# Second step of a sparse-attention graph layer: five rounds of top values, a slope from a law, and small steps moved to GpSimd

## Chip, cores and metric

One core of one Trainium2 chip runs the whole program. The metric is device time in microseconds (us) from launch to end. The engines are PE (TensorE matmul), PEld (its weight loads), DVE (VectorE), ACT (ScalarE), POOL (GpSimd) and SP (SyncE, which issues DMAs).

## What is computed

For 3327 nodes with 256 features, x is normalised and rectified to h. Then two steps of two diffusions are run over h: one along a sparse adjacency matrix, one along an attention matrix that keeps, in each row, the largest probabilities until their sum reaches 0.9.

```python
for n in range(STEPS):                       # STEPS = 2
    q = Xa @ W1.T @ W2.T; k = Xa @ W3.T
    probs = softmax(q @ k.T)
    A = probs where (sum of the larger ones in the row) < TOP_P else 0     # TOP_P = 0.9
    A = A / A.sum(-1)
    Xf = R @ Xf                              # R = (adj + I), rows normalised
    Xa = A @ Xa
    Z = Z + Xf @ U1[n].T + Xa @ U2[n].T
out = x + layernorm(h + Z)
```

## The kernel before

The nodes are padded to 3328 and cut into 26 tiles of 128 rows. A tile's row of exponentials `e` is 128 x 3328 in float32. Two steps, one after the other, walk over the tiles; in each iteration i of a step's loop, tile i+1 is guessed, tile i is settled and tile i-1 is multiplied, so that several tiles are in flight.

No row is sorted. For each tile, and for each of its 128 rows at once:

- `weights` makes logits on PE (L600) and exponentials on ACT (L604, L608).
- `measured_twice` (second step; `measured_once` in the first) guesses the value at which the larger part of the row's sum is 0.9. A first guess comes from `guessed` (ACT, L620 to L625). Three passes of ACT over `e` (L633, through the helper `through`) measure how much lies under the guess: a Relu, a Sign, and a Sign against a second guess. Between and behind them stand short operations on 128 x 1 columns of a small tile `g` (`col(k)`): on ACT L674 and L675, L687 and L688, L702 to L704; on GpSimd L676 to L678, L689 to L692, L697 and L698, L708 to L712; on DVE L685 and L686, L699 and L700, L706 and L707. L699 reads column 14, which L689 writes. The last exponential, L714 on ACT, gives the final guess, `col(16)`.
- `settle` takes the values under that guess into `w`, with their sum `d2` (L729, on DVE over all 3328 columns). `need` (L730) is what is still to be dropped. The eight largest of each of 20 segments of `w` become 160 candidates (L734). Rounds of a maximum of eight and a replacement (L741, L743) give the largest 48 of them in order in the second step, 40 in the first; a running sum and a comparison with `need` (L748 to L753) give the exact cut. L763 masks `e` with it and sums the row into `ra`, whose reciprocal is L764.
- `Sums` transposes the masked `e` (PE L809, copies by ACT at L811) and multiplies it with the features (`pa`, L823).
- `spread`, `fetched` and `diffuse` gather up to five neighbours' rows by indirect DMAs that GpSimd issues (`xg`, L921) and multiply them (`pr`, L929).
- `finish` (second step) adds up the tile with `ra` (L953, DVE), takes mean and variance (L458, L459), computes the inverse deviation on GpSimd (L465, L466, the second a power) and `nm` (L961), asks for `x` (`xr`, L958, on SP), and then scales, shifts and adds on GpSimd (L968 to L971) and stores (L973).

If any row's cut isn't proved to be right by the candidates (`prove`), a flag makes the program run `search_graph_layer`, which searches by bits, over everything again.

The order of the instructions is written by hand. All of these are generators; an iteration has seven slots, and a string for each slot names by letters which generator goes one stage further: m `measured_twice` of tile i+1, n the same of the tile before (its last stage), d `settle` of tile i, c its last stages an iteration later, f `finish`, g the next gather, s `spread`, w and q `weights`, l the laws. `PLAN[1]` has the second step's strings, `OPEN` those of its first iterations, `LAST` those of its last. At the end every engine's instructions but those of SP in the second step are tied to the order of the text. In the second step's plan the third stage of `finish` (the `xr` load, L465, L466, L961) stands in slot 5, ahead of the part of the guess in slot 6, and one gather stands at the end of slot 6, four in slot 3.

Of the kernel before, what the change touches and what calls it, by code (L numbers as in the profile page):

```python
# [13 lines left out]
AF = mybir.ActivationFunctionType  # L14
ALU = mybir.AluOpType
# [15 lines left out]

SCALE = 1.9
BITS = 27
FIRST = 2.0 ** -7
assert 0.1 * SCALE / N > 2.0 ** -15


# [1 line left out]
def search_graph_layer(  # L39
# [13 lines left out]
    nc = tc.nc  # L53
# [94 lines left out]
    def nucleus(es, z):  # L148
        n = len(es)
        thr = small.tile([P, 2], F32, tag="thr", name="thr")  # L150
        cand = small.tile([P, 2], F32, tag="cand", name="cand")
        ncand = small.tile([P, 2], F32, tag="ncand", name="ncand")
        over = small.tile([P, 2], F32, tag="over", name="over")
        cnt = small.tile([P, 2], F32, tag="cnt", name="cnt")
        mass = small.tile([P, 2], F32, tag="mass", name="mass")
        low = small.tile([P, 2], I32, tag="low", name="low")
        candi = cand.bitcast(I32)
        nc.vector.tensor_scalar(thr, z, TOP_P, None, ALU.mult)
        nc.vector.memset(cand, FIRST)
        for k in range(BITS - 1, -1, -1):  # L160

            nc.vector.tensor_scalar(ncand, cand, -1.0, None, ALU.mult)
            for a in range(n):
                ja = scan.tile([P, NP], U8, tag="ja", name="ja")
                nc.scalar.activation(ja, es[a], AF.Relu, bias=ncand[:, a : a + 1],
                                     accum_out=over[:, a : a + 1])
                jv = scan.tile([P, NP], U8, tag="jv", name="jv")
                nc.vector.tensor_scalar(jv, es[a], cand[:, a : a + 1], None, ALU.is_ge, ALU.add,
                                        accum_out=cnt[:, a : a + 1])
            nc.vector.tensor_tensor(mass, cand, cnt, ALU.mult)  # L170
            nc.vector.tensor_tensor(mass, mass, over, ALU.add)
            nc.vector.tensor_tensor(low, mass, thr, ALU.is_lt)

            nc.vector.tensor_scalar(low, low, k, (1 << k) >> 1,
                                    ALU.logical_shift_left, ALU.bitwise_or)
            nc.vector.tensor_tensor(candi, candi, low, ALU.bitwise_xor)

        rc = small.tile([P, 2], F32, tag="rc", name="rc")  # L180
        nc.vector.reciprocal(rc, cand)
        nc.vector.tensor_scalar(ncand, cand, -1.0, None, ALU.mult)
        lim = small.tile([P, 2], F32, tag="lim", name="lim")
        for a in range(n):
            c = slice(a, a + 1)
            e = es[a]
            nc.vector.scalar_tensor_tensor(e, e, cand[:, c], e, ALU.is_ge, ALU.mult,
                                           accum_out=mass[:, c])
            eq = scan.tile([P, NP], U8, tag="jv", name="eq")
            nc.vector.tensor_scalar(eq, e, cand[:, c], None, ALU.is_equal)  # L190
            nth = scan.tile([P, NP], I16, tag="nth", name="nth")
            nc.vector.tensor_tensor_scan(nth, eq, eq, 0.0, ALU.add, ALU.max)

            nc.vector.tensor_sub(lim[:, c], thr[:, c], mass[:, c])
            nc.vector.scalar_tensor_tensor(lim[:, c], lim[:, c], rc[:, c], nth[:, NP - 1 : NP],
                                           ALU.mult, ALU.add)
            nc.vector.tensor_scalar(lim[:, c], lim[:, c], 1.0, None, ALU.add)
            nc.vector.scalar_tensor_tensor(eq, nth, lim[:, c], eq, ALU.is_ge, ALU.mult)
            nc.vector.scalar_tensor_tensor(e, eq, ncand[:, c], e, ALU.mult, ALU.add)
# [114 lines left out]
LNBIG = 69.0  # L314
SEG = 168
NSEG = -(-NP // SEG)
ROUNDS = (5, 6)
PG = (0.72168716, 3.51308980, -3.48705157)
PK = (3.57528079, -2.54929187, 0.86603878)
OFFSET = (18.0, 14.0)  # L320
TOPK = 8 * max(ROUNDS)
LNY = 0.25 * math.log(0.72)

# [5 lines left out]
HALVES = 7  # L329
FIRST = 8 * P  # L330
CUT = 4
# [14 lines left out]
def guess_graph_layer(ctx, tc, x, adj, w1t, w2t, w3t, u1t, u2t, ln_g, ln_b, out, flag):  # L346
    nc = tc.nc
# [14 lines left out]
    V, G, S, PE = nc.vector, nc.gpsimd, nc.scalar, nc.tensor  # L362
# [46 lines left out]
    half = const.tile([P, 4], F32, tag="half", name="half")  # L409
# [218 lines left out]
    def con(k):  # L628
        return one[:, k : k + 1]
# [38 lines left out]
    def measured_twice(r):  # L668
        e, ms = r["e"], r["ms"]

        col = guessed(r, small.tile([P, 18], F32, tag="g", name="g"))
        S.activation(col(1), col(0), AF.Exp, scale=-1.0, bias=con(5))  # L674
        S.activation(col(11), col(2), AF.Square, bias=con(4))  # L675
        G.tensor_scalar(col(11), col(11), ms(5), ms(6), ALU.mult, ALU.add)  # L676
        G.tensor_scalar(col(5), col(1), OFFSET[1], None, ALU.mult)
        G.tensor_scalar(col(7), col(3), ms(3), ms(8), ALU.mult, ALU.add)  # L678
        yield
        oa = small.tile([P, 3], F32, tag="oa", name="oa")  # L680
        through(e, AF.Relu, col(9), -1.0, oa[:, 0:1])
        yield
        through(e, AF.Sign, col(9), -1.0, oa[:, 1:2])
        yield
        V.tensor_scalar(col(3), oa[:, 1:2], float(NP), col(9), ALU.add, ALU.mult)  # L685
        V.tensor_scalar(col(4), col(3), 0.5, oa[:, 0:1], ALU.mult, ALU.subtract)  # L686
        S.activation(col(6), col(4), AF.Ln, scale=col(1), bias=con(2))  # L687
        S.activation(col(13), col(6), AF.Exp, scale=col(11), bias=col(7))  # L688
        G.tensor_scalar(col(14), col(13), col(9), 0.25, ALU.add, ALU.mult)  # L689
        G.tensor_scalar(col(10), col(13), col(5), 1.0, ALU.mult, ALU.add)  # L690
        G.tensor_scalar(col(8), r["Z"], -0.1, col(4), ALU.mult, ALU.add)
        G.tensor_scalar(col(6), col(6), col(11), col(7), ALU.mult, ALU.add)  # L692
        yield
        through(e, AF.Sign, col(13), -1.0, oa[:, 2:3])
        yield
        d1 = col(17)
        G.tensor_scalar(col(0), oa[:, 2:3], NP - 61.0, BIG, ALU.is_gt, ALU.mult)  # L697
        G.tensor_scalar(col(0), r["Z"], 0.035, col(0), ALU.mult, ALU.add)  # L698
        V.tensor_scalar(col(15), oa[:, 2:3], oa[:, 1:2], col(14), ALU.subtract, ALU.mult)  # L699
        V.tensor_scalar(d1, col(15), col(4), 0.0, ALU.add, ALU.max)  # L700

        S.activation(col(2), d1, AF.Abs, scale=col(1), bias=con(1))  # L702
        S.activation(col(2), col(2), AF.Ln, scale=0.2, bias=col(10))
        S.activation(col(3), d1, AF.Ln, scale=col(1), bias=con(2))  # L704

        V.tensor_scalar(col(12), col(4), d1, 1.0e-30, ALU.subtract, ALU.add)  # L706
        V.reciprocal(col(12), col(12))  # L707
        G.tensor_scalar(col(12), col(12), col(8), 0.7, ALU.mult, ALU.max)  # L708
        G.tensor_scalar(col(11), col(12), 1.5, col(11), ALU.min, ALU.mult)
        G.tensor_tensor(col(2), col(3), col(2), ALU.subtract)  # L710
        G.tensor_scalar(col(15), d1, col(0), LNBIG, ALU.is_lt, ALU.mult)
        G.tensor_tensor(col(6), col(6), col(15), ALU.add)  # L712
        yield
        S.activation(col(16), col(2), AF.Exp, scale=col(11), bias=col(6))  # L714
        yield

    def measured(step, r):
# [5 lines left out]
    def settle(step, t, r):  # L723
        e, col, Z = r["e"], r["col"], r["Z"]
        n = 8 * ROUNDS[step]
        d2 = small.tile([P, 1], F32, tag="d2", name="d2")
        need = small.tile([P, 1], F32, tag="need", name="need")
        w = scan.tile([P, NP], F32, tag="w", name="w")
        V.scalar_tensor_tensor(w, e, col(16), e, ALU.is_lt, ALU.mult, accum_out=d2)  # L729
        V.tensor_scalar(need, Z, -0.1, d2, ALU.mult, ALU.add)  # L730
        yield
        cand = small.tile([P, NSEG * 8], F32, tag="cand", name="cand", bufs=1)
        for s in range(NSEG):
            V.max(cand[:, 8 * s : 8 * s + 8], w[:, s * SEG : min(NP, (s + 1) * SEG)])  # L734
# [26 lines left out]
            V.tensor_tensor(ra, ra, rb, ALU.add)  # L761
        else:
            V.scalar_tensor_tensor(e, e, at(1), e, ALU.is_ge, ALU.mult, accum_out=ra)  # L763
        V.reciprocal(ra, ra)  # L764
        yield
        V.tensor_tensor(cum[:, :n], dr[:, :n], b, ALU.mult)
        V.tensor_reduce(at(2), cum[:, :n], AX.X, ALU.max)

# [357 lines left out]
    def refetch(t):  # L1126
# [7 lines left out]


    PLAN = (("gmdsssa", "gmcdsssa", "edawwpg", "gmsdga", "gmspdea", "ohgdawwqg", "gehmgq"),
            ("llcmss", "lnms", "lwwnfd", "lcmdsssgggg", "fdsmwqdf", "llmdf", "lmwdg"))

    LAST = {NT - 1: ("cfss", "cn", "nd", "sss", "fddddddsf", "f", ""), NT: ("c", "", "", "ff", "ff", "fv", "f"),
            NT + 1: ("fv", "f", "", "", "f", "f", "f")}  # L1140
# [3 lines left out]
             2: ("gmdsssa", "gmcdsssga", "gedawwpg", "gmsdga", "gmspdea", "ohgdawwqg", "gehmgq")}  # L1144
    OPEN = {-1: ("llcmss", "lnms", "lwwnfd", "lcmdsssggggg", "fmgdswqdf", "llmdf", "lmwfdm"),
            0: ("cmssggg", "nms", "wwnfd", "cmdsss", "fdsmgwqdf", "mdf", "mwd"),
            1: ("cmss", "nms", "wwnfd", "cmdsssgggg", "fdsmwqdf", "mgdf", "mwdg")}
    OPEN[2] = OPEN[3] = OPEN[1]
    spacing = itertools.chain(spaced((0, 1)), *(spaced((t,)) for t in range(2, NT)))
    fetching = itertools.chain(*(refetch(t) for t in range(NT)))  # L1150
# [130 lines left out]
```

## Times and profile before

| what | us |
|---|---|
| median of 3 runs | 1354.68 |
| lowest, highest | 1349.92, 1356.13 |
| the profiled execution | 1350.64 |
| its span (first to last instruction) | 1348.9 |
| mean granted TensorE clock | 0.982 |
| PE busy in the span | 1268.1 (94%) |
| DVE busy | 1186.8 (88%) |
| ACT busy | 1081.0 (80%) |
| POOL busy | 997.2 (74%) |

The page divides the span into 40 slices of 33.7 us; the first step ends at about 742 us, with slice 22, and the second fills the rest. A digit is the busy share of a slice in tenths. The page's groups name line, engine, operation, what is written and read, and how often. Timeline lines give start and duration in us, engine, line, operation, operands, and in brackets the idle time ahead of it and what ended it. The ends of matmuls are modelled in the profile, so for PE the spacing of starts is read and not the durations; durations on POOL are rough.

Some of the groups in the second step, from 780 to 1220 us of the span, mean of one:

| line, engine | operation | ns |
|---|---|---|
| L763 DVE | mask and row sum, 3328 columns | 3685 |
| L729 DVE | values under the guess, 3328 columns | 3677 |
| L741 DVE | maximum of eight out of 160 | 323 |
| L743 DVE | replacement of eight in 160 | 309 |
| L730, L706 DVE | column operations | 214 |
| L707, L764 DVE | reciprocal of a column | 164 |
| L633 ACT | one pass over `e` | 3069 |
| L702 ACT | Abs of a column | 387 |
| L466 POOL | power of a column | 579 |
| L690 POOL | column operation | 262 |
| L921 POOL | one indirect DMA (mean; median of all 954) | 1155 |

### The profile page before, as it was taken

The page shows a single profiled execution, that of the slowest core. Times are in us where ns is not written, and L with a number is a line of the kernel's source. Part 1 is how long each engine was busy: PE and PEld are TensorE (multiplying, and loading weights), DVE is VectorE, ACT ScalarE, POOL GpSimd, SP SyncE. Part 2 cuts the span into 40 slices and gives each one's busy share as a digit, 9 for nine tenths or more (in the row PEclk, how much of TensorE's full clock was granted, in tenths as well). Part 3 has the DMA queues.
Part 4 walks back from the last instruction along what each step waited for, and adds up shares of the span by engine and source line. Part 5 has one row for each costly group of instructions (what it writes and reads, how often), then busy time and mean ns, then how long its engine had stood idle before and what let it go on. Part 6 is the DMA issues. An engine that isn't in the chain of part 4 may idle for free.

```text
span 1348.9 us, 22270 instructions
## 1 busy us (share of the span) xinstructions
PE 1268.1 (94%) x6495; PEld 976.0 (72%) x6495; DVE 1186.8 (88%) x3637; ACT 1081.0 (80%) x2368; POOL 997.2 (74%) x1399
## 2 busy tenths in 40 slices
PE   5989899999999999999999579999999999999985
PEld 4635687877778777787877457777777777777774
DVE  6877899999999999999990689899998999999993
ACT  5475788798888879888863789899998999999841
POOL 5114788888878878887873578888888888888832
PEclk9999999999999999999999779999999999999998
DMA  8644545455454544445332212221212222122200
GB/s 277 221 157 141 160 136 144 134 144 147 133 153 133 140 138 142 144 135 152 106 104 86 75 55 60 78 89 54 91 59 85 62 82 90 52 91 64 81 21 24
DMA packets 92645, 149.79 MB, mean 111 GB/s; under 512 B 15425, under 2 KB 59072, under 8 KB 92512
## 3 DMA queue, kind: packets, MB, share of 16 engines
q1 hardware_dynamic: 75056, 105.37, 24.6%
q0 software_dynamic: 16640, 42.69, 12.1%
q8 instruction: 54, 0.88, 0.3%
q14 instruction: 79, 0.65, 0.2%
q10 hardware_dynamic: 816, 0.20, 0.1%
HBM read 120.93 MB, written 27.28 MB: 110 GB/s over the span
## 4 chain that ended last, share of the span: by engine, by line
PE 51%; DVE 20%; ACT 12%; POOL 11%; issue 3%; DMA 2%; SPq 0%; POOLq 0%; DVEq 0%; ACTq 0%
PE pa L823 22%; ACT ja L633 7%; PE pl L600 7%; PE pt L809 6%; PE pr L929 5%; POOL xg L921 5%; DVE w L729 4%; PE pz L942 3%; DVE cand L734 3%; DVE e L763 3%; PE pz L1011 2%; POOL g L676 2%; DVE bb L741 1%; DVE cand L743 1%; ACT e L604 1%
## 5 line engine op out<-in xcount | busy, mean ns | idle before, releaser
L823 PE MATMUL pa<-xw,eT 128*128 128x256 f32 x1352 | 323.6, 384 | 3.6 <-DVE s L953 3.6
L633 ACT ACTIVATE ja<-e,g 128x3328 uint8<-128x3328 f32 x106 | 325.7, 3072 | 0.1
L823 PE MATMUL pa<-x,eT 128*128 128x256 f32 x1352 | 323.1, 380 | 0.0
L823 PEld LDWEIGHTS pa<-xw,eT 128*128 128x128 f32 x1352 | 250.7, 190 | 52.5 <-issue 14.4
L823 PEld LDWEIGHTS pa<-x,eT 128*128 128x128 f32 x1352 | 243.7, 191 | 25.8
L734 DVE MAX8 cand<-w 128x8 f32<-128x168 f32 (+1 forms) x1040 | 253.7, 319 | 0.0
L811 ACT COPY eT<-pt 128x512 f32<-128x512 f32 (+1 forms) x364 | 199.5, 555 | 48.8 <-PE pt L809 47.7
L921 POOL DMA_INDIRECT xg<-bx,index x130 | 188.7, 1451 | 54.7 <-issue 24.4
L900 POOL DMA_INDIRECT ac<-in_adj,index x130 | 162.9, 1253 | 63.8 <-issue 28.2
L809 PE MATMUL pt<-ident,e 128*128 128x128 f32 x1144 | 176.6, 277 | 17.3 <-DVE e L760 9.4
L809 PEld LDWEIGHTS pt<-ident,e 128*128 128x128 f32 x1144 | 139.8, 144 | 60.5 <-issue 36.0
L921 POOL DMA_INDIRECT xg<-vx,index x130 | 152.5, 1173 | 34.3 <-issue 30.3
L729 DVE SCALAR_TENSOR_TENSOR w<-e,g 128x3328 f32<-128x3328 f32 x44 | 162.7, 3698 | 3.1 <-ACT g L714 3.0
L929 PE MATMUL pr<-xg,ac 128*128 128x257 f32 (+1 forms) x520 | 141.0, 395 | 8.4 <-DVE s L1119 6.8
L763 DVE SCALAR_TENSOR_TENSOR e<-e,rec 128x3328 f32<-128x3328 f32 x40 | 148.3, 3707 | 0.6
L604 ACT ACTIVATE e<-pl 128x832 f32<-128x832 f32 x132 | 112.9, 859 | 27.3 <-PE pl L600 21.9
L929 PEld LDWEIGHTS pr<-xg,ac 128*128 128x128 f32 x520 | 93.9, 194 | 34.0 <-issue 14.1
L600 PE MATMUL pl<-both,qT 64*128 64x416 f32 x416 | 93.0, 546 | 9.3 <-ACT e L604 7.0
L741 DVE MAX8 bb<-cand 128x8 f32<-128x160 f32 x286 | 92.7, 324 | 6.4
L853 DVE TENSOR_REDUCE fm<-at 128x4 f32<-128x512 f32 (+1 forms) x133 | 84.7, 637 | 13.3 <-DMA at<-in_adj 13.3
L600 PE MATMUL pl<-after,qT 64*128 64x416 f32 x416 | 95.4, 552 | 0.5 <-ACT e L604 0.5
L633 ACT ACTIVATE ja<-x,g 128x3328 uint8<-128x3328 f32 x24 | 73.7, 3070 | 0.0
(260 smaller groups left out, 2129.8 us busy)
## 6 DMA issues: line engine op xcount, KB each, us to landing
at<-in_adj SPq DMA_DIRECT2D x114, 256.0 KB
cx<-ac SPq DMA_DIRECT2D x26, 384.0 KB
ac<-cx SPq DMA_DIRECT2D x26, 384.0 KB
wide<-in_adj SPq DMA_DIRECT2D x8, 832.0 KB
e<-in_adj SPq DMA_DIRECT2D x6, 832.0 KB
own<-bx SPq DMA_DIRECT2D x26, 128.5 KB
x<-in_x SPq DMA_DIRECT2D x13, 256.0 KB
xr<-in_x SPq DMA_DIRECT2D x26, 128.0 KB
```

The costliest lines, as they stand in the source:

```text
L600: PE.matmul(pl[:, a, :wd], qT[p, :], keys_of(step, a).rearrange("p a b -> p (a b)")[:, c : c + wd], start=True, stop=True)
L604: S.activation(e.rearrange("p (a n) -> p a n", a=2)[:, :, c : c + wd], pl[:, :, :wd], AF.Exp, accum_out=za[:, n : n + 1])
L633: S.activation(ja, e, f, bias=guess, scale=sign, accum_out=total)
L729: V.scalar_tensor_tensor(w, e, col(16), e, ALU.is_lt, ALU.mult, accum_out=d2)
L734: V.max(cand[:, 8 * s : 8 * s + 8], w[:, s * SEG : min(NP, (s + 1) * SEG)])
L763: V.scalar_tensor_tensor(e, e, at(1), e, ALU.is_ge, ALU.mult, accum_out=ra)
L809: PE.transpose(pt[:, j, :], e[:, (j0 + j) * P : (j0 + j + 1) * P], ident)
L811: S.copy(eT[:, :w, :], pt[:, :w, :])
L823: PE.matmul(self.pa, eT[:, c - 4 * k, :], self.xa[:, j, :], start=c == 0, stop=c == NT - 1)
L900: G.indirect_dma_start(out=ac[:, k, :], out_offset=None, in_=rows, in_offset=bass.IndirectOffsetOnAxis(ap=index[:, t, k : k + 1], axis=0), ...
L921: G.indirect_dma_start(out=xg[:, k, :w], out_offset=None, in_=rows, in_offset=bass.IndirectOffsetOnAxis(ap=index[:, t, k : k + 1], axis=0))
L929: PE.matmul(pr[:, :w], ac[:, k, :], own if k == KT - 1 else xg[:, k, :w], start=k == 0, stop=k == KT - 1)
```

## The change

All of it is in the second step.

- `ROUNDS[1]` goes from 6 to 5: the cut is looked for among 40 candidates. `OFFSET[1]` goes from 14 to 24, which sets how far above the expected cut the guess is put.
- The slope with which the guess is corrected is no longer measured (L706 and L707 on DVE, L708 and L709 on GpSimd, with the column of L691) but computed from the law's column 11 by two new operations on GpSimd behind L678, -0.4 col(11)^2 + 0.5 col(11). ACT's Abs (L702) goes; the first of its two logarithms is taken of column 10, which doesn't depend on d1. Three operations on GpSimd stand in place of L708 to L712.
- `need` (L730) and `ra`'s reciprocal (L764, now a power of -1) are computed on GpSimd in the second step, at the beginning of the following stage of `settle`: both in slot 3, behind `finish`'s scaling (L968 to L971, slot 2) and ahead of that slot's four gathers.
- In the second step's plan the third stage of `finish` moves from slot 5 to slot 6, behind the guess's operations there and ahead of the slot's gather.

`FIRST` in the other program is renamed to `LOWEST`.

```diff
--- before.py
+++ after.py
...
@@ -314,10 +314,10 @@
 LNBIG = 69.0
 SEG = 168
 NSEG = -(-NP // SEG)
-ROUNDS = (5, 6)
+ROUNDS = (5, 5)
 PG = (0.72168716, 3.51308980, -3.48705157)
 PK = (3.57528079, -2.54929187, 0.86603878)
-OFFSET = (18.0, 14.0)
+OFFSET = (18.0, 24.0)
 TOPK = 8 * max(ROUNDS)
 LNY = 0.25 * math.log(0.72)
 
@@ -676,6 +676,8 @@
         G.tensor_scalar(col(11), col(11), ms(5), ms(6), ALU.mult, ALU.add)
         G.tensor_scalar(col(5), col(1), OFFSET[1], None, ALU.mult)
         G.tensor_scalar(col(7), col(3), ms(3), ms(8), ALU.mult, ALU.add)
+        G.tensor_scalar(col(12), col(11), -0.4, 0.5, ALU.mult, ALU.add)
+        G.tensor_tensor(col(12), col(12), col(11), ALU.mult)
         yield
         oa = small.tile([P, 3], F32, tag="oa", name="oa")
         through(e, AF.Relu, col(9), -1.0, oa[:, 0:1])
@@ -688,7 +690,6 @@
         S.activation(col(13), col(6), AF.Exp, scale=col(11), bias=col(7))
         G.tensor_scalar(col(14), col(13), col(9), 0.25, ALU.add, ALU.mult)
         G.tensor_scalar(col(10), col(13), col(5), 1.0, ALU.mult, ALU.add)
-        G.tensor_scalar(col(8), r["Z"], -0.1, col(4), ALU.mult, ALU.add)
         G.tensor_scalar(col(6), col(6), col(11), col(7), ALU.mult, ALU.add)
         yield
         through(e, AF.Sign, col(13), -1.0, oa[:, 2:3])
@@ -699,19 +700,13 @@
         V.tensor_scalar(col(15), oa[:, 2:3], oa[:, 1:2], col(14), ALU.subtract, ALU.mult)
         V.tensor_scalar(d1, col(15), col(4), 0.0, ALU.add, ALU.max)
 
-        S.activation(col(2), d1, AF.Abs, scale=col(1), bias=con(1))
-        S.activation(col(2), col(2), AF.Ln, scale=0.2, bias=col(10))
+        S.activation(col(2), col(10), AF.Ln)
         S.activation(col(3), d1, AF.Ln, scale=col(1), bias=con(2))
-
-        V.tensor_scalar(col(12), col(4), d1, 1.0e-30, ALU.subtract, ALU.add)
-        V.reciprocal(col(12), col(12))
-        G.tensor_scalar(col(12), col(12), col(8), 0.7, ALU.mult, ALU.max)
-        G.tensor_scalar(col(11), col(12), 1.5, col(11), ALU.min, ALU.mult)
-        G.tensor_tensor(col(2), col(3), col(2), ALU.subtract)
+        G.tensor_scalar(col(2), col(2), col(12), col(6), ALU.mult, ALU.subtract)
         G.tensor_scalar(col(15), d1, col(0), LNBIG, ALU.is_lt, ALU.mult)
-        G.tensor_tensor(col(6), col(6), col(15), ALU.add)
-        yield
-        S.activation(col(16), col(2), AF.Exp, scale=col(11), bias=col(6))
+        G.tensor_tensor(col(2), col(15), col(2), ALU.subtract)
+        yield
+        S.activation(col(16), col(3), AF.Exp, scale=col(12), bias=col(2))
         yield
 
     def measured(step, r):
@@ -727,8 +722,11 @@
         need = small.tile([P, 1], F32, tag="need", name="need")
         w = scan.tile([P, NP], F32, tag="w", name="w")
         V.scalar_tensor_tensor(w, e, col(16), e, ALU.is_lt, ALU.mult, accum_out=d2)
-        V.tensor_scalar(need, Z, -0.1, d2, ALU.mult, ALU.add)
-        yield
+        if not step:
+            V.tensor_scalar(need, Z, -0.1, d2, ALU.mult, ALU.add)
+        yield
+        if step:
+            G.tensor_scalar(need, Z, -0.1, d2, ALU.mult, ALU.add)
         cand = small.tile([P, NSEG * 8], F32, tag="cand", name="cand", bufs=1)
         for s in range(NSEG):
             V.max(cand[:, 8 * s : 8 * s + 8], w[:, s * SEG : min(NP, (s + 1) * SEG)])
@@ -761,8 +759,11 @@
             V.tensor_tensor(ra, ra, rb, ALU.add)
         else:
             V.scalar_tensor_tensor(e, e, at(1), e, ALU.is_ge, ALU.mult, accum_out=ra)
-        V.reciprocal(ra, ra)
-        yield
+        if not step:
+            V.reciprocal(ra, ra)
+        yield
+        if step:
+            G.tensor_tensor(ra, ra, half[:, 2:3], ALU.pow)
         V.tensor_tensor(cum[:, :n], dr[:, :n], b, ALU.mult)
         V.tensor_reduce(at(2), cum[:, :n], AX.X, ALU.max)
 
@@ -1134,7 +1135,7 @@
 
 
     PLAN = (("gmdsssa", "gmcdsssa", "edawwpg", "gmsdga", "gmspdea", "ohgdawwqg", "gehmgq"),
-            ("llcmss", "lnms", "lwwnfd", "lcmdsssgggg", "fdsmwqdf", "llmdf", "lmwdg"))
+            ("llcmss", "lnms", "lwwnfd", "lcmdsssgggg", "fdsmwqdf", "llmd", "lmwfdg"))
 
     LAST = {NT - 1: ("cfss", "cn", "nd", "sss", "fddddddsf", "f", ""), NT: ("c", "", "", "ff", "ff", "fv", "f"),
             NT + 1: ("fv", "f", "", "", "f", "f", "f")}
@@ -1144,7 +1145,7 @@
              2: ("gmdsssa", "gmcdsssga", "gedawwpg", "gmsdga", "gmspdea", "ohgdawwqg", "gehmgq")}
     OPEN = {-1: ("llcmss", "lnms", "lwwnfd", "lcmdsssggggg", "fmgdswqdf", "llmdf", "lmwfdm"),
             0: ("cmssggg", "nms", "wwnfd", "cmdsss", "fdsmgwqdf", "mdf", "mwd"),
-            1: ("cmss", "nms", "wwnfd", "cmdsssgggg", "fdsmwqdf", "mgdf", "mwdg")}
+            1: ("cmss", "nms", "wwnfd", "cmdsssgggg", "fdsmwqdf", "mgd", "mwfdg")}
     OPEN[2] = OPEN[3] = OPEN[1]
     spacing = itertools.chain(spaced((0, 1)), *(spaced((t,)) for t in range(2, NT)))
     fetching = itertools.chain(*(refetch(t) for t in range(NT)))
```

More of the change, by code (lines that the diff above doesn't have):

```diff
@@ L33 @@
 BITS = 27
-FIRST = 2.0 ** -7
+LOWEST = 2.0 ** -7
 assert 0.1 * SCALE / N > 2.0 ** -15
@@ L158, in nucleus @@
         nc.vector.tensor_scalar(thr, z, TOP_P, None, ALU.mult)
-        nc.vector.memset(cand, FIRST)
+        nc.vector.memset(cand, LOWEST)
         for k in range(BITS - 1, -1, -1):
```

## The prediction

> **What bounds the kernel now.** I read first the page's slices, then windows over the second step, then one settled tile engine by engine in the timeline. Nothing in the first step changes, so the case lies in slices 23 to 40.
>
> ```profile
> PE   5989899999999999999999579999999999999985
> DVE  6877899999999999999990689899998999999993
> ACT  5475788798888879888863789899998999999841
> POOL 5114788888878878887873578888888888888832
> ```
>
> All four engines are busy there, so shares decide nothing. The next lines are windows: length, then busy time of PE, weight loads, DVE, ACT and POOL (instructions), clock, DMA. The first runs over the settled tiles (cut at each tile's first `pa` matmul): 21 tiles, 21.30 us each. The second is one of them.
>
> ```profile
> 831.39:1278.68 447.29, 441.66 (x2267) 343.31 (x2266) 417.61 (x1240) 418.83 (x817) 384.39 (x546) 1.00 0.25 75
> 1153.00:1173.97 20.97, 20.97 (x109) 16.37 (x108) 19.82 (x60) 20.00 (x40) 18.39 (x27) 1.00 0.25 75
> ```
>
> Most tiles take 20.97 to 21.05; two stumble (22.85 from 852, 24.25 from 1023), each with one of 21.6 behind it. In a smooth tile PE is full: its 52 `pa` matmuls start 0.216 us apart, as in the first step where the chain is PE alone, and its one wait is 0.09 to 0.12 us at the first transpose, for L763. PE's own tile is thus 20.87. I call L763 (mask e, sum ra) the cut pass and L729 (values under the guess into w) the guess pass. A loop of DVE and ACT is just as long: from 897 to 999 the chain of waits alternates between these two, at 21.0 a tile. From 1200 to 1275 it names GpSimd, so that comes next, in one tile:
>
> ```profile
> 1220.16 0.24 POOL L677 TENSOR_SCALAR g<-g 128x1 f32<-128x1 f32 x1
> ...
> 1228.65 0.28 POOL L689 TENSOR_SCALAR g<-g 128x1 f32<-128x1 f32 x1
> ...
> 1230.35 0.58 POOL L466 TENSOR_TENSOR rstd<-rstd,half 128x1 f32<-128x1 f32 x1
> 1231.04 0.26 POOL L961 TENSOR_SCALAR nm<-mv,rstd 128x1 f32<-128x1 f32 x1
> ...
> 1233.37 0.19 POOL L712 TENSOR_TENSOR g<-g 128x1 f32<-128x1 f32 x1
> 1233.73 4.35 POOL L921 DMA_INDIRECT xg<-vx,index  x1 [0.17 <-issue]
> 1238.14 2.95 POOL L676 TENSOR_SCALAR g<-g,law 128x1 f32<-128x1 f32 x1
> 1241.15 0.24 POOL L677 TENSOR_SCALAR g<-g 128x1 f32<-128x1 f32 x1
> ```
>
> and DVE beside it:
>
> ```profile
> 1229.54 0.27 DVE L699 TENSOR_SCALAR g<-oa,g 128x1 f32<-128x1 f32 x1 [0.38 <-ACT ja L633]
> ...
> 1233.39 3.69 DVE L763 SCALAR_TENSOR_TENSOR e<-e,rec 128x3328 f32<-128x3328 f32 x1
> 1237.01 0.08 DVE L763 DVE_READ_ACCUMULATOR e<-e,rec 128x1 f32 x1
> 1237.12 0.16 DVE L764 RECIPROCAL ra<-ra 128x1 f32<-128x1 f32 x1
> 1237.20 3.67 DVE L729 SCALAR_TENSOR_TENSOR w<-x,g 128x3328 f32<-128x3328 f32 x1
> ```
>
> GpSimd's queue has no pause. A gather (0.95 us alone) that starts 0.34 us into the cut pass takes 4.35, and L676 (0.34 alone) started in the guess pass ends 0.21 us behind it. Operations that started up to 0.09 us into a pass go through. So a pass shuts GpSimd out, and between two passes one waiting operation slips through. The chain's 4.35 and 2.95 are therefore ends of DVE's passes. The stumbles are the same thing at a worse moment: at 1021 L711, a part of the guess, fell into the cut pass,
>
> ```profile
> 1021.26 3.66 POOL L711 TENSOR_SCALAR g<-g 128x1 f32<-128x1 f32 x1
> ```
>
> and ACT's exponential L714, and with it the guess pass, came late.
>
> **What the Trainium skill says.** "SBUF — State Buffer", section "Who interferes with whom": a VectorE instruction with two SBUF inputs and a GpSimd instruction that reads SBUF exclude each other, and whoever issues first makes the other wait. The trace agrees (waits of 2.6 to 3.4 us). The same section infers that a `tensor_tensor` doesn't stop a GpSimd DMA's descriptor generation; here, under a two-input pass, the gather goes from 0.95 to 4.35, and first-step gathers issued within guess passes end some 0.83 us behind them. "Perfetto Trace Analysis", section "GPSIMD Engine Instruction": time GpSimd by the spacing of starts, not by reported durations; I do. Its section "Identifying the Most-Contended Engine": matmul busy share is no measure of headroom; hence the spacing of matmuls above.
>
> **The change, part by part**, for a settled tile.
>
> DVE loses one round of top values, 0.77 by spacing; L706 and L707, 0.45 (the next maximum follows L700 by 0.13, as one follows L686, instead of 0.58); `need` 0.21; `ra`'s reciprocal 0.1; and about 0.06 on four operations with 40 instead of 48 columns: 1.6 in all. From L699 to the cut pass, 3.85 becomes 2.57. On ACT the Abs goes and the first Ln no longer waits for d1: the work behind comes 0.68 sooner. The DVE-ACT loop falls by 0.9 to 1.6, below PE.
>
> GpSimd gains, ahead of L689: the slope's two operations behind L678, spacings 0.41+0.41+0.17 against 0.31, +0.66; and `ra` (a power like L466) and `need` behind L971, 0.75+0.60+0.44 against 0.88, +0.91. Nothing hides these, since its queue is full: L677 to L689 grows from 8.49 to 10.06. `ra` waits for the cut pass and `need` for the guess pass, both over by then; behind them queue the four gathers and L689. `need` is read 7 us later and `ra` in the next tile by L953, so DVE doesn't wait for these; were `ra` late, L953 would hold DVE and, through `pa`, PE. The gathers' rows are read by PE 20 us after issue. L971's store goes out later on SP by what GpSimd slips, about 2 us, and the loads of `xr`, `sx`, `cx` and `own` stand behind it in the same order as before; the first of them is needed some 14 us on. It loses L691 and swaps L708 to L712 for three operations, 1.0 less, but behind L689, where DVE doesn't wait for it.
>
> DVE waits for L689: L699 reads its column 14. Now L689 ends 9.05 us behind the guess pass's end, and L699 starts at 9.66, after 0.38 of waiting for ACT. Let L677 come w after that end. Then L689 starts at w+10.06, takes 0.28, reaches DVE in about 0.07, 2.57 later the cut pass starts, and both passes take 3.69+0.03+3.67. The loop is w+20.37.
>
> What is w? `rstd`, its power and `nm` (L465, L466, L961) now stand behind the guess. From L689 to L466 I count spacings of 0.24+0.30+0.41+0.36+0.37+0.41+0.37+0.17+0.32 = 2.95. The cut pass starts at 2.92: L466 just gets through, `nm` would start at 3.64, is shut out and takes the gap between the passes, and the fifth gather falls into the guess pass and ends 0.83 behind it; L676 follows at 0.05 and L677 at 0.40 more: w = 1.28. The period is 21.65, against 20.87 for PE and 20.1 for DVE and ACT. GpSimd becomes the bound. The stumbles go, since the guess is done at 2.65.
>
> Sums. Start-up (GpSimd has no finished tile yet): 1.0 at the first guess, 1.3 before the first cut pass, 1.7 from there to the second: -4.0. Settled: a first tile of 20.4, 20 of 21.65, and 2.6 for one pause of GpSimd's queue as at 1012: 456.0 against 447.4, +8.6. End: 0.6 for L712, which runs into the cut pass at 1275, and 1.4 for each of the last two tiles: -3.4. Total +1.2. The profiled execution took 1350.64 (span 1348.9 and 1.7 around it), so 1351.8. It lies 4 us under the median 1354.68 of three runs that spread over 6; from the middle of all four, 1353, I say 1354.
>
> **Rivals.** (1) GpSimd keeps up and PE binds. For it: PE's tile is 20.87, and the stumbles, 6 us, vanish. Against it: `nm` would have to start before the cut pass, 0.6 us earlier than counted. Then 21x20.87 = 438.3: -9.1-4.0-3.4 = -16.5, about 1337. A half-way case, with `nm` just in time by a later cut pass, has period 21.25 and gives 1346. (2) The power L466 misses the cut pass's start, from 0.1 us into it; it has 0.06 to spare. Then it takes the gap, `nm` waits out the guess pass and the gather stands wholly behind: w about 1.7, period 22.1, 465.0 against 447.4, +17.6-7.4 = +10: about 1363, slower. The gap of 0.03 instead of 0.12, with `ra` gone from DVE, could do the same. (3) The guess fails for a row and the second program runs. Worked through on the given inputs, the formulas put the cut within the first 36 of 40 values, so hardly; far over 1400.
>
> **How the numbers follow.** Forecast 0.37, keeping up or half-way 0.34, missed power 0.27, failing 0.02. A measurement can tell 0.5%, 6.8 us, from no change. The added spacings are uncertain by 0.3 us a tile: of the forecast 0.04 ends faster and 0.03 slower, of the half-way case 0.01 is no change, and of the missed power 0.02. Faster 0.37, same 0.33, slower 0.30. The forecast's own range is 1347 to 1360; with most of (1) and (2) it is 1337 to 1366.
>
> **What would show it.** Right: DVE idle before L699's successor with GpSimd as releaser, about 2 us a tile; every fifth gather lasting over 3 us inside the guess pass; PE idle 0.8 a tile; no stumbles. Wrong: tiles of 20.9 with PE never idle (rival 1), or the power lasting over 3 us (rival 2). DVE's busy time per tile should fall by about 1.5 in any case; if not, the count of removed work is wrong.

## The result and the profile after

The changed kernel takes 1358.30 us (median of 20 runs, 1354.05 to 1365.89), the kernel before 1353.31 (20 runs, 1349.60 to 1358.70): ratio 1.0047, 95% interval 1.0031 to 1.0063. It is slower by half a per cent; the forecast was no change. The 1358.30 lies inside the forecast's own range, 1347 to 1360, but with 20 runs of each kernel the interval of the ratio leaves out 1. Runs of either kernel fall into two groups some 6 us apart, and since in the traces of this case the first step, which no kernel here changes, takes either 738 to 740 or 745 to 748 us, medians of a few runs are rough to some us. So I compare the second step of the one profiled execution of each kernel, counted from its first law matmul, L525, to the end: 609.51 us before, 618.16 after.

First the page's slices of the changed kernel, tenths busy:

```profile
DVE  6877799999999999999990698888887888878893
...
POOL 5204788888878878887873588889888888888872
```

DVE has come down from 9 to 8 in the second half, POOL has not. The share of the chain that ended last tells more. Before:

```profile
PE 51%; DVE 20%; ACT 12%; POOL 11%; issue 3%; DMA 2%; SPq 0%; POOLq 0%; DVEq 0%; ACTq 0%
```

After:

```profile
PE 53%; POOL 25%; ACT 7%; DVE 7%; issue 5%; DMA 2%; SPq 0%; POOLq 0%; DVEq 0%; ACTq 0%
```

Windows of the changed kernel, with the columns as before (length, busy PE, weight loads, DVE, ACT, POOL): the 21 settled tiles, and then one tile of each of the two lengths that occur.

```profile
830.52:1292.77 462.25, 442.16 (x2267) 343.41 (x2266) 387.91 (x1087) 411.04 (x793) 405.60 (x563) 1.00 0.24 73
939.39:961.49 22.10, 21.05 (x109) 16.37 (x108) 18.52 (x54) 19.66 (x38) 19.46 (x28) 1.00 0.24 70
983.64:1005.28 21.64, 21.06 (x110) 16.37 (x108) 18.09 (x51) 19.27 (x38) 19.17 (x26) 1.00 0.22 70
```

The 21 tiles take 462.25 instead of 447.29. (All these windows, those ahead of the result too, begin at one `pa` matmul of a tile and end 21 tiles on at the same one, but it is not the tile's first, as I had written, and not the same one in every kernel; from first to first the stretches are 462.8 and 447.3.) DVE is busy for 29.7 less (1.41 a tile), POOL for 21.2 more (an operation that a pass holds up counts as busy). PE, which was full, now has a gap of 0.75 us (short tile) or 1.23 (long) at the first transpose, by the spacing of its starts. Cut at the cut pass (now L761), the tiles are 21.66 to 21.68 (6 of them) or 22.11 to 22.13 (13), and two of 23.1.

What makes a tile long shows on GpSimd. Its timeline, a long tile and then the beginning of a short one:

```profile
941.25 0.24 POOL L465 TENSOR_SCALAR rstd<-mv 128x1 f32<-128x1 f32 x1
941.57 4.07 POOL L466 TENSOR_TENSOR rstd<-rstd,half 128x1 f32<-128x1 f32 x1
945.74 3.24 POOL L962 TENSOR_SCALAR nm<-mv,rstd 128x1 f32<-128x1 f32 x1
949.15 1.10 POOL L922 DMA_INDIRECT xg<-vx,index  x1 [0.17 <-issue]
...
950.74 0.24 POOL L677 TENSOR_SCALAR g<-g 128x1 f32<-128x1 f32 x1
...
960.73 0.28 POOL L691 TENSOR_SCALAR g<-g 128x1 f32<-128x1 f32 x1
...
963.68 0.58 POOL L466 TENSOR_TENSOR rstd<-rstd,half 128x1 f32<-128x1 f32 x1
964.36 3.12 POOL L962 TENSOR_SCALAR nm<-mv,rstd 128x1 f32<-128x1 f32 x1
967.65 4.28 POOL L922 DMA_INDIRECT xg<-vx,index  x1 [0.17 <-issue]
...
972.41 0.24 POOL L677 TENSOR_SCALAR g<-g 128x1 f32<-128x1 f32 x1
```

and DVE in the long tile:

```profile
938.92 0.27 DVE L700 TENSOR_SCALAR g<-oa,g 128x1 f32<-128x1 f32 x1 [2.48 <-issue]
...
941.52 3.69 DVE L761 SCALAR_TENSOR_TENSOR e<-e,rec 128x3328 f32<-128x3328 f32 x1
...
945.13 3.68 DVE L724 SCALAR_TENSOR_TENSOR w<-e,g 128x3328 f32<-128x3328 f32 x1
```

The 2.48 us ahead of L700 are DVE's wait for GpSimd. The trace names no releaser here ("issue"), but L700 starts 0.30 to 0.31 us behind L691 in every settled tile, where before it started 0.7 us or more behind L689 in all but one.

In the long tile the power L466 starts 0.05 us behind the cut pass's start and is shut out until that pass ends; it takes the gap between the passes, `nm` waits out the guess pass, and the gather and L677 follow: w, from the guess pass's end (948.81) to L677, is 1.93. In the short tile (cut pass from 963.64, guess pass to 970.95) the power starts 0.04 behind and gets through; `nm` takes the gap, the gather ends 0.98 behind the guess pass: w = 1.46. The rest of the loop is the same in both: L677 to L691 10.00, to L700 0.31, to the cut pass 2.60, both passes 7.29: w + 20.20. That gives 21.66 and 22.13.

Over all 20 settled tiles with the power near the pass, it got through in 6, with starts 0.039 to 0.048 us behind the pass's, and was shut out in 14, with starts 0.047 to 0.057.

### The profile page after: what moved, and what is told of

It is laid out like the page before. It is cut to its first block, busy times and chain, and to the rows that moved or that the text cites. A ratio compares the mean times of both kernels' runs of the same rounds, so it can differ in the third digit from the quotient of the medians.

```text
span 1363.1 us, 22094 instructions
## 1 busy us (share of the span) xinstructions
PE 1271.8 (93%) x6495; PEld 977.3 (72%) x6495; DVE 1149.6 (84%) x3455; ACT 1070.6 (79%) x2342; POOL 1025.3 (75%) x1425
## 4 chain that ended last, share of the span: by engine, by line
PE 53%; POOL 25%; ACT 7%; DVE 7%; issue 5%; DMA 2%; SPq 0%; POOLq 0%; DVEq 0%; ACTq 0%
PE pa L824 23%; POOL xg L922 7%; PE pl L600 7%; PE pt L810 6%; PE pr L930 5%; POOL nm L962 4%; POOL rstd L466 4%; ACT ja L633 4%; PE pz L943 3%; PE pz L1012 3%; DVE cand L732 1%; DVE w L724 1%; POOL s L970 1%; PE pk L1056 1%; POOL xr L971 1%
## 5 line engine op out<-in xcount | busy, mean ns | idle before, releaser
L761 DVE SCALAR_TENSOR_TENSOR e<-e,rec 128x3328 f32<-128x3328 f32 x40 | 147.3, 3682 | 0.6
L739 DVE MAX8 bb<-cand 128x8 f32<-128x160 f32 x260 | 84.3, 324 | 5.5
L962 POOL TENSOR_SCALAR nm<-mv,rstd 128x1 f32<-128x1 f32 x26 | 71.9, 2767 | 2.7
```

The source lines that it names most:

```text
L962: G.tensor_scalar(nm, mv[:, 0:1], rstd, -1.0, ALU.mult, ALU.mult)
```

## Experiments

My theory: GpSimd's loop is the bound, and what is left of it behind the guess pass is set by which operation of GpSimd meets which pass. Rivals: the other order of `finish` costs the time by itself; the slope's operations do; DVE's or ACT's own work sets the tile; the amount of GpSimd work counts and not its place. Lines are the changed kernel's unless said otherwise. All ratios are to the kernel before; "settled tile" is the mean of the 21 (from the first `pa` matmul of one to the first of the 21st behind it). The ratios are of medians; second step and tiles are of one profiled execution each.

| kernel | ratio (95%) | second step | settled tile |
|---|---|---|---|
| before | 1 | 609.51 | 21.30 |
| changed | 1.0047 (1.0031 to 1.0063) | 618.16 | 22.04 |
| both row-sum steps on DVE | 0.9905 (0.9875 to 0.9935) | 596.85 | 20.99 |
| slope behind L693 | 1.0092 (1.0065 to 1.0119) | 624.42 | 22.34 |
| epsilon on DVE | 1.0012 (0.9993 to 1.0031) | 611.46 | 21.67 |
| six rounds | 1.0002 (0.9982 to 1.0023) | 609.38 | 21.45 |
| order of before | 1.0057 (1.0035 to 1.0079) | 620.39 | 22.03 |
| no nm | 1.0062 (1.0036 to 1.0088) | 614.58 | 21.90 |
| row sums on DVE, slope late | 0.9970 (0.9955 to 0.9984) | 607.25 | 21.44 |
| the same, order of before | 0.9897 (0.9868 to 0.9925) | 597.09 | 20.96 |
| before, row sums on GpSimd | 1.0170 (1.0144 to 1.0196) | 632.83 | 22.38 |

**Both row-sum steps back on DVE.**

```diff
-        if not step:
-            V.tensor_scalar(need, Z, -0.1, d2, ALU.mult, ALU.add)
+        V.tensor_scalar(need, Z, -0.1, d2, ALU.mult, ALU.add)
         yield
-        if step:
-            G.tensor_scalar(need, Z, -0.1, d2, ALU.mult, ALU.add)
...
-        if not step:
-            V.reciprocal(ra, ra)
+        V.reciprocal(ra, ra)
         yield
-        if step:
-            G.tensor_tensor(ra, ra, half[:, 2:3], ALU.pow)
```

> The changed kernel with need and ra's reciprocal back on DVE, all else as changed. GpSimd-loop theory: the stretch from L677 to L691 on GpSimd falls from 10.0 to about 9.1 us, so the loop falls from 21.65/22.1 to 20.75/21.2 a tile and PE's 20.87 begins to bind: tiles of 20.9 to 21.3, about 21 x 1.0 = 20 us less than the changed kernel, some 1338. If the loss came from the other order (the third stage of finish behind the guess) or from the slope's two operations alone, nothing moves: 22.1 a tile, 1358. If DVE's work bounded the tile, the 0.3 us that it gets back makes it slower: 22.4, about 1365.

Measured: 1339.08 us. Its settled tiles by windows:

```profile
832.22:1271.28 439.06, 437.32 (x2259) 344.33 (x2258) 392.68 (x1127) 410.52 (x793) 386.05 (x525) 1.00 0.25 77
```

From first to first `pa` matmul the stretch is 440.8, 22.0 less than the changed kernel's 462.8, and PE is full again (busy 437.32 of the 439.06): most tiles take 20.86 or 20.87. L677 to L691 takes 8.94 (958.18 to 967.12) instead of 10.00, and for DVE's wait this trace does name GpSimd:

```profile
967.42 0.27 DVE L700 TENSOR_SCALAR g<-oa,g 128x1 f32<-128x1 f32 x1 [0.59 <-POOL g L691]
```

Two operations of 0.58 and 0.27 us, moved, cost 1.4% (1.0047 against 0.9905). DVE has 4.8 us more to do, and nothing comes of it. The order, the slope and the DVE rivals fall as main causes.

**One part alone, on the kernel before**: the same two operations moved to GpSimd, six rounds and all else as before (the reverse of the diff above).

> The kernel before with one part of the change alone: need and ra's reciprocal on GpSimd in the second step (six rounds, measured slope and order stay). Theory of GpSimd's loop: GpSimd's column 14 (L689 of before) comes 1.06 us later in every tile, DVE waited 0.6 us at most behind it, so L699 is 0.7 us late and the tile grows from 21.0 to about 21.7; the guess's last operations run into the cut pass as often as before or more. 0.7 x 21 = 15 us more, some 1368; DVE's 0.3 us less are worth nothing. If GpSimd's small steps are hidden beside DVE, as their place between other work suggests, 1350 to 1354.

Measured: 1377.46 us, more than expected. Cut at the first `pa` matmul, tiles alternate between 21.60 and 23.10. In every second tile DVE waits for GpSimd, L699 starting 0.31 behind L689; without a stumble the sum around the loop would be 0.33 + 9.57 + 0.31 + 3.87 + 7.29 = 21.37, near the expected 21.7. But these tiles stumble besides, which the expectation had left at "as often as before or more", and in the tile behind each of them L699 waits for ACT instead and comes 1.05 behind L689. GpSimd and DVE in a stumble, with this kernel's lines (L711 is the guess, L766 the cut pass, L729 the guess pass):

```profile
1124.85 3.66 POOL L711 TENSOR_SCALAR g<-g 128x1 f32<-128x1 f32 x1
```

```profile
1124.64 3.70 DVE L766 SCALAR_TENSOR_TENSOR e<-e,rec 128x3328 f32<-128x3328 f32 x1
...
1129.23 3.91 DVE L729 SCALAR_TENSOR_TENSOR w<-x,g 128x3328 f32<-128x3328 f32 x1 [0.89 <-ACT g L714]
```

L711 starts 0.21 us into the cut pass, is shut out until it ends, and the guess pass comes 0.89 late behind ACT's exponential. The moved steps are thus the costly part on either kernel, 1.4 and 1.7%; the rest of the change gains 1%.

**The power surely ahead of the cut pass**: epsilon (L465) is added on DVE, right behind mean and variance.

```diff
         mv = spread_of(y)
+        V.tensor_scalar(mv[:, 1:2], mv[:, 1:2], LN_EPS, None, ALU.add)
         yield
...
-        G.tensor_scalar(rstd, mv[:, 1:2], LN_EPS, None, ALU.add)
-        G.tensor_tensor(rstd, rstd, half[:, :1], ALU.pow)
+        G.tensor_tensor(rstd, mv[:, 1:2], half[:, :1], ALU.pow)
```

> The changed kernel with the addition of epsilon (L465) on DVE right behind the mean and variance, some 5 us ahead of need, instead of on GpSimd. The power L466 then starts 0.3 us ahead of the cut pass and not 0.05 behind its start. Theory of the race: the power gets through in every tile, all settled tiles are of the shorter kind, 21.65, none of 22.1: 14 x 0.46 = 6 us less, some 1352. If the two tile lengths come from something else (the gather's memory, the clock), both remain and the time stays at 1358.

Measured: 1356.82 us and a second step 6.7 shorter than the changed kernel's. Apart from the opening and one pause of the gathers' queue at 1025 (23.07), every tile takes 21.61 to 21.65; none is long. GpSimd there (L465 is the power, the cut pass starts at 962.85):

```profile
962.44 0.59 POOL L465 TENSOR_TENSOR rstd<-mv,half 128x1 f32<-128x1 f32 x1
963.13 3.54 POOL L962 TENSOR_SCALAR nm<-mv,rstd 128x1 f32<-128x1 f32 x1
966.84 4.27 POOL L921 DMA_INDIRECT xg<-vx,index  x1 [0.17 <-issue]
```

This is the case that I had forecast, made to happen: 18 of the 21 settled tiles take 21.61 to 21.64 by cut passes, where I had forecast 21.65. The whole stretch from the third cut pass to the 24th takes 455.96, and my sum was 456.0; so close a match is luck, since a stumble of 1.4 in the opening, which I had not foreseen, makes up for a pause of the gathers of 1.45 where I had put 2.6. The ratio, 1.0012, can't be told from the forecast "no change".

**More work on DVE**: the sixth round back.

```diff
-ROUNDS = (5, 5)
+ROUNDS = (5, 6)
```

> The changed kernel with a sixth round of maximum and replacement put back on DVE (48 instead of 40 candidates; the law and the offset stay). It lies between L701 and the cut pass, 0.7 us. GpSimd-loop theory: the cut pass starts 0.7 us later, so the power L466 and perhaps nm (L962) pass ahead of it. With both through, the gather fills the cut pass, L676 takes the gap, w falls from 1.5-1.9 to about 0.6: 0.6 + 20.2 + 0.7 = 21.5 a tile, 12 us less than the changed kernel although more work is done, some 1346. With nm shut out w is 1.46: 22.4, 1364. If the tile is bounded by DVE's sum of work, 0.7 x 21 = 15 us more: 1373.

Measured: 1352.66 us. The smooth tiles are 21.34 to 21.39, shorter than either length of the changed kernel, with DVE's 0.8 us more per tile between L701 and the cut pass. GpSimd (cut pass 960.52, guess pass 964.13 to 967.81):

```profile
960.86 4.33 POOL L922 DMA_INDIRECT xg<-vx,index  x1 [0.17 <-issue]
965.25 2.82 POOL L676 TENSOR_SCALAR g<-g,law 128x1 f32<-128x1 f32 x1
968.16 0.24 POOL L677 TENSOR_SCALAR g<-g 128x1 f32<-128x1 f32 x1
```

Power and `nm` (960.43) are through, the gather fills the cut pass, L676 takes the gap, and L677 comes 0.35 behind the guess pass. 0.35 + 10.00 + 0.31 + 3.42 + 7.29 = 21.37. This speaks most clearly against DVE as the bound: the removed round is worth less than nothing here. The second step is 8.8 shorter than the changed kernel's, somewhat less than the expected 12.

**The slope's operations moved behind L693.**

```diff
         G.tensor_scalar(col(7), col(3), ms(3), ms(8), ALU.mult, ALU.add)
-        G.tensor_scalar(col(12), col(11), -0.4, 0.5, ALU.mult, ALU.add)
-        G.tensor_tensor(col(12), col(12), col(11), ALU.mult)
...
         G.tensor_scalar(col(6), col(6), col(11), col(7), ALU.mult, ALU.add)
+        G.tensor_scalar(col(12), col(11), -0.4, 0.5, ALU.mult, ALU.add)
+        G.tensor_tensor(col(12), col(12), col(11), ALU.mult)
```

> The changed kernel with the slope's two GpSimd operations moved from behind L678 to behind L693, where GpSimd then waits for ACT or DVE anyway. GpSimd-loop theory: L677 to L691 falls by 0.6 to about 9.4 us, the guess's L698 to L707 start as much behind L691 as the two operations take (0.4 to 0.6 us), and so does the power L466: it is now surely shut out by the cut pass, w stays near 1.9. Tiles of 21.5, about 0.6 x 21 = 12 us less, some 1346; if the late guess parts run into the cut pass, nothing is won (22.1, 1358). If place and not amount of the work mattered little (DVE or PE bound), 1358.

Measured: 1366.51 us, 22.33 a tile: slower, which I had not expected. L677 to L691 did fall, by 0.44. But everything behind L693 is 0.46 us later against the cut pass, and that is enough (cut pass 964.30, guess pass 967.91 to 971.59):

```profile
964.49 3.59 POOL L465 TENSOR_SCALAR rstd<-mv 128x1 f32<-128x1 f32 x1
968.16 3.87 POOL L466 TENSOR_TENSOR rstd<-rstd,half 128x1 f32<-128x1 f32 x1
972.14 0.26 POOL L962 TENSOR_SCALAR nm<-mv,rstd 128x1 f32<-128x1 f32 x1
```

Now L465 takes the gap, the power waits out the guess pass, and `nm` and the gather stand wholly behind it: w = 2.55. My expectation had taken the power, and not L465, to be the first that is shut out (w near 1.9).

**The order of before in the changed kernel.**

```diff
-            ("llcmss", "lnms", "lwwnfd", "lcmdsssgggg", "fdsmwqdf", "llmd", "lmwfdg"))
+            ("llcmss", "lnms", "lwwnfd", "lcmdsssgggg", "fdsmwqdf", "llmdf", "lmwdg"))
...
-            1: ("cmss", "nms", "wwnfd", "cmdsssgggg", "fdsmwqdf", "mgd", "mwfdg")}
+            1: ("cmss", "nms", "wwnfd", "cmdsssgggg", "fdsmwqdf", "mgdf", "mwdg")}
```

> The changed kernel with the order of before: the third stage of finish (L465, L466, L962) back ahead of the guess's L698 to L707, four gathers and all moved operations as changed. Theory of GpSimd's loop: L691 comes as late as in the changed kernel (10.0 us behind L677), the three operations add 1.35 us ahead of L698, so L706 and L707 meet the cut pass: one is shut out through it, the exponential L709 and with it the guess pass come 0.8 us late in every tile. 21.6 to 22.4 a tile, 1348 to 1365: the order alone is no cure. If the move of the third stage is what costs, tiles fall to 21.3 and below: 1342 or less.

Measured: 1360.44 us, 22.00 to 22.03 in most tiles. GpSimd's L706, ahead of the exponential, meets the cut pass (from 1120.90) in nearly every tile, and the guess pass starts 0.89 late:

```profile
1121.03 3.73 POOL L706 TENSOR_SCALAR g<-g 128x1 f32<-128x1 f32 x1
```

So the order is neither cause nor cure: with GpSimd late, what stands behind L693 meets the passes in either order.

**One operation fewer behind the guess**: the scaling subtracts the mean itself.

```diff
-        nm = small.tile([P, 1], F32, tag="nm", name="nm")
-        G.tensor_scalar(nm, mv[:, 0:1], rstd, -1.0, ALU.mult, ALU.mult)
...
-            G.tensor_scalar(y, y, rstd, nm, ALU.mult, ALU.add)
+            G.tensor_scalar(y, y, mv[:, 0:1], rstd, ALU.subtract, ALU.mult)
```

> The changed kernel without nm (L962): the scaling subtracts the mean and multiplies by the inverse deviation in one operation, so that one operation fewer stands behind the guess, 0.4 us of work. Theory that a pass shuts GpSimd out and one operation takes the gap: where the power gets through, the gather fills the cut pass, L676 takes the gap, w is 0.6 and the tile 20.9; where the power is shut out, it takes the gap and the gather ends 0.83 behind the guess pass: w 1.3, tile 21.5. 12 to 25 us less than the changed kernel, 1333 to 1346, several times what the removed operation lasts (0.4 x 21 = 8). If only the amount of work counted: 21.7, 1350.

Measured: 1362.59 us; the interval overlaps that of the changed kernel, while the second step of its profiled execution is 3.6 shorter, so whether it gains anything stays unclear. The expected 12 to 25 us didn't come. Tiles are 21.40 where the power gets through (w = 0.34) and 22.50 where it is shut out (w = 1.44): w is near the expected 0.6 and 1.3, but L677 to L691 grew to 10.86, because the scaling became slow:

```profile
1120.12 1.26 POOL L967 TENSOR_SCALAR s<-s,mv,rstd 128x256 f32<-128x256 f32 x1
```

In the changed kernel the same scaling as multiply and add, L969, takes 0.56. What makes the difference, the operation or its operands, was not tried.

**Both row sums on DVE and the slope late**, the first and the fourth edit together:

> need and ra's reciprocal on DVE and the slope's two operations behind L693: the GpSimd work ahead of L691 is that of before again, while DVE keeps the removed round and reciprocal. Theory: GpSimd's loop is w + 18.9, with w up to 2.5 because L465 or L466 may be shut out: 20.8 to 21.4, against PE's 20.87. Between 1334 (all at PE's pace, as with need and ra alone on DVE) and 1345. If the late slope operations cost nothing, 1336.

Measured: 1348.42 us, above the expected 1334 to 1345. L677 to L691 is down to 8.5, 0.4 below the kernel with the row sums alone, and the time is 9 us above it: L465 starts 0.09 or 0.19 behind the cut pass, is shut out in nearly every tile and w is 2.54, so the loop is 21.49 in most tiles and binds; in the kernel with the row sums alone the power mostly gets through, the loop is 20.8 and PE binds.

**The same with the order of before**, so that of the change only the fifth round, the law, the offset and ACT's two logarithms are left:

> As the kernel with need and ra on DVE and the slope late, and with the third stage of finish back in slot 5: only the fifth round, the law and the offset remain of the change. Theory: L691 is now early enough that GpSimd waits 3 us for ACT's third pass, and the third stage and the slope lie in that wait; behind the guess stands only the gather, w at most 1.3; GpSimd's loop is below 20.5 and PE binds in all tiles, without stumbles: 20.87 x 21, about 9 us less than before in the middle part and 7 at the ends: 1336, the fastest. If the order matters by itself or the removed DVE work brings nothing, 1350.

Measured: 1338.20 us, tiles of 20.86 and 20.87, PE full. GpSimd now does the third stage of `finish` while it waits for ACT's third pass (the cut pass is at 1118.79):

```profile
1115.69 0.57 POOL L466 TENSOR_TENSOR rstd<-rstd,half 128x1 f32<-128x1 f32 x1
...
1118.59 1.12 POOL L916 DMA_INDIRECT xg<-vx,index  x1 [0.17 <-issue]
1120.91 1.78 POOL L676 TENSOR_SCALAR g<-g,law 128x1 f32<-128x1 f32 x1 [1.21 <-ACT g L675]
```

GpSimd waits 1.21 us for ACT where it had no pause, so its loop has slack. This kernel and the one with the row sums alone on DVE beat the kernel before by 1% and the changed one by 1.4 to 1.5%; the two can't be told apart.

## Why the prediction went wrong

**What held.** The frame: the row sums and the slope go onto a full GpSimd queue, DVE waits for it, GpSimd becomes the bound. Its terms: DVE 1.6 less a tile (1.41); L699 to the cut pass 2.57 (2.60); L677 to L689, now L691, 10.06 (10.00; the row sums take 1.06 where I had 0.91, the slope 0.45 where I had 0.66); PE idle 0.8 a tile (0.75 in short tiles). The short tile is the forecast tile, 21.65, though by two small errors that cancel: w is 1.46 and not 1.28 (the gather ends 0.98 behind the pass, not 0.83), and the rest 20.20 and not 20.37. That an exclusive hold decides, as "SBUF — State Buffer", section "Who interferes with whom", in the Trainium skill says, agrees with the traces: the power takes 4.07 us instead of 0.58 where it meets a pass.

**The step that failed**: "The cut pass starts at 2.92: L466 just gets through", with "0.06 to spare". The count was good: L466 was to come 0.03 us behind the cut pass's start and came 0.039 to 0.057 behind it. The allowance was not. "Operations that started up to 0.09 us into a pass go through" rested on gathers of the first step, whose starts up to 0.086 did; of column operations the trace of before had one that got through behind a pass's start, L710 at 0.034, and the next, L712 at 0.142, was shut out. For the power the limit is 0.046 to 0.048, so there was nothing to spare and 14 of 20 tiles fell on the other side. That is rival 2's tile: 22.1 forecast, 22.12 measured, again with errors that cancel (w 1.93 and not 1.7, the rest 20.20 and not 20.37). With epsilon on DVE, where the power starts 0.4 us ahead of the pass, the short tile came in every smooth tile. That edit also takes one operation out of GpSimd's queue behind the guess, but the short tile keeps its length with it (21.63 against 21.67), so what it changes is on which side the power falls.

**The sum**, by cut passes, in the profiled executions. The start-up to the second one: 63.87 from L525 instead of 67.46, -3.6 (forecast -4.0). The tile behind it: +1.0, not foreseen. The next 21: 463.82 against 447.39, +16.4 (forecast +8.6): 13 shut-out powers at 0.46 (the 14th falls behind the stretch) are 6.0 of the difference, a tile of 23.09 1.4, a first tile of 21.67 for 20.4 1.3, and a shorter pause of the gathers, 1.5 for 2.6, takes back 1.1; together 7.6 of 7.8. The end: -5.2 (forecast -3.4). In all +8.65, where the forecast was +1.2 and rival 2 said +10.

**"The stumbles go"** was wrong in the opening. There the plan puts a gather between L693 and L698, and L706 meets the cut pass at 809.06 and again at 852.7. In the changed kernel:

```profile
806.89 0.96 POOL L922 DMA_INDIRECT xg<-vx,index  x1 [0.15 <-issue]
...
809.06 3.62 POOL L706 TENSOR_SCALAR g<-g 128x1 f32<-128x1 f32 x1
```

The changed kernel's longer tiles there are the 1.0 and the 1.4 above.

**The rivals.** Rival 1 would have needed `nm` ahead of the cut pass; with the sixth round it got there, at 21.36 a tile and not PE's 20.87, since the round itself lies in the loop. Rival 2 is what happened in two tiles of three; I gave it 0.27 although its margin was 0.06 us, less than the uncertainty of 0.3 us a tile that I stated for the same sum. Slower, which came, had the least of the three chances, 0.30. Rival 3 didn't happen. Whether the later stores on SP cost anything was not tried.

## What to carry to other kernels

Before moving small operations to another engine, follow that engine's queue through the tile: two operations of 0.58 and 0.27 us cost 1.4% of this kernel because GpSimd had no pause and DVE waited behind it; back on DVE they cost nothing. Where two engines exclude each other, place the work by the other's long passes: what meets a pass costs its rest, so taking work out elsewhere can make things worse (slope late) and adding some can help (six rounds). And where a forecast hangs on a margin smaller than the error of the sum, put the chance near even and take the limit from the same operation, not from another's.

## What the runs showed of the hardware

- The limit for the power is sharp and small: in the three kernels where the power L466 comes close to the cut pass's start (changed, row sums on DVE, no nm) it got through in 36 of 60 tiles, all with recorded starts up to 0.048 us behind the pass's, and was shut out in 24, all from 0.046 on. L465, at 0.087 and later, was always shut out, but at 0.046 it got through once (six rounds). There is no one limit for all small operations: L705 was shut out once at a recorded start 0.023 us ahead of a pass's (order of before) and once 0.010 behind it (slope late), L706 at 0.018 (row sums on DVE, slope late, order of before). The gathers' limit is later: recorded starts up to 0.096 got through, and two at 0.093 and 0.109 were shut out.
- Between two passes that follow each other with no gap in DVE's records, or with only the reciprocal's 0.12 us between them, exactly one waiting operation of GpSimd gets in, in each of some 200 such pairs in the traces here.
- On GpSimd, a `tensor_scalar` of 128x256 with subtract and multiply takes 1.257 us, with multiply and add 0.555 (medians of 25 each).
